# A cross-attention and mixture-of-experts kernel: first units' loads and copies in a new order, and scores and copies moved forward in the units without a value projection

## The chip, the cores and the metric

The kernel runs on one core of a Trainium2 chip. The metric is device time in microseconds (us) of one execution. One profiled execution is there too, with a record of every instruction. The engines are PE (TensorE; PEld is its weight load), ACT (ScalarE), DVE (VectorE), POOL (GpSimd) and SP, which here only issues DMAs. Each engine executes its own list in order.

## The reference, cut to what matters

```python
x = x + _L0_xattn_ref(_layernorm(x, axis=-1), ctx_1024, ctx_1024, L0_xattn_WQ, L0_xattn_WK, L0_xattn_WV, L0_xattn_Wfc, L0_xattn_bfc)
x = x + _L0_ffn_ref(_layernorm(x, axis=-1), L0_ffn_gate_w, L0_ffn_Wg, L0_ffn_Wu, L0_ffn_Wd, L0_ffn_Ws_g, L0_ffn_Ws_u, L0_ffn_Ws_d)
```

There are 32 sequences of 100 tokens with 512 features. `_L0_xattn_ref` projects the normalised x to queries and the first 100 rows of the context to keys and values, takes a causal softmax in 16 heads of 32 features, multiplies it with the values, and projects the result with `Wfc`. `_L0_ffn_ref` sends the 12 best tokens of each sequence to each of 16 experts and adds a shared expert. The change lies in the attention alone; the second line is unchanged.

## The kernel before, in words

**Units.** The attention runs in 32 units. Unit u stands for super-block sb = u // 4 (four sequences, 400 tokens) and feature chunk c = u % 4 (128 features, four heads). The main loop (L561) issues units 0 to 28; `last_units` (L421) writes out 29 to 31 together with the start of the feed-forward part. All five engines' orders are written out by hand: the order of the calls is the order of the instructions on each engine.

**Three units at once.** Iteration u works on three units: the query projection `qproj(u)` of its own, scores and softmax of a = u - 1, and transposes and value product of back = u - 2. For a: `scores(a)` (L259, PE, into the one score tile, `sc`), `sm_max` (L270, DVE) in two halves of two sequences each, `sm_sub` (L279, POOL), `sm_exp` (L285, ACT), `sm_sum` (L290 and L291, DVE) and `sm_mul` (L296, POOL). For back: `p_turn` (L302, PE transposes of one sequence's probabilities into a PSUM tile `ms`), `p_keep` (L307, ACT, copy of that tile to `pt`), and `values` (L317, PE, into another `ms` tile). `y_keep` (L104 on ACT, L105 on DVE) copies the value product out one iteration later and writes it to `yD`. There are two `ms` buffers: the transposes of sequences 2 and 3 take those of sequences 0 and 1, the value product takes that of sequence 2, and the next unit's second transpose takes that of the value product.

**Keys and values beside it.** The context comes in nine blocks j of 2 or 3 times 128 rows. Blocks 0 and 1 are projected in `prologue` (L332), the seven others in iterations 1 to 28, four iterations a block: each has one key projection (`kproj`, copied by `kkeep`, L223, to `kD` in memory) and the first three also have a value projection (`vproj`, copied by `vkeep`, L203, to `vD`). The fourth, u = 4, 8, ..., 28, is a unit without values. `ctx_split` (L138 on ACT, L139 on POOL, tile `cxl`) prepares a later block. `kload` (L229) and `vload` (L234) read keys and values back; `xt_load`, `xt_split`, `x_load`, `x_stats` and `x_rstd` (L161, L162 on POOL) prepare queries and the normalisation of a later super-block. The projections share two PSUM buffers `kv`, so each waits for the copy of the one two before it.

**Order in a unit without values, before.** ACT: `q`, exponential of half 0 of a, `pt` of sequences 0 and 1, exponential of half 1, `pt` of sequences 2 and 3, `kk`. PE: `scores(a)`, `qproj`, transposes 0 and 1, `kproj`, transposes 2 and 3, `values`. POOL: two `sm_sub`, `x_rstd` (every fourth unit), two `sm_mul`, `cxl`, and then the next unit's `sm_sub`.

**Queue of loads.** SP issues nearly all DMAs in the order of the program, and an issue waits for the completion of the DMA eight places before it, besides its own data. `last_units` uses the output projection `fc` (L56, with tiles `yh` and `yl`, loaded by `load_y`, L1048) from its first unit on; `vload` of the last super-block stands in `last_units` (L437).

Of the kernel before, what the change touches and what calls it, by code (L numbers as in the profile page):

```python
# [18 lines left out]
NC4 = D // 128  # L19
# [41 lines left out]
def attention(tc, K, F):  # L61
    nc = tc.nc
    with ExitStack() as ctx, ExitStack() as kvctx:
# [37 lines left out]
        nsb = K.nsb  # L101
# [31 lines left out]
        def ctx_split(j, d, eng=nc.gpsimd):  # L133
            n = KVB[j] * 128
            cr = cur.pop(("cr", j, d))
            h = cxp.tile([128, KMAX], FR, name="cxh")
            l = cxp.tile([128, KMAX], FR, name="cxl")
            nc.scalar.copy(h[:, 0:n], cr[:, 0:n])  # L138
            eng.tensor_tensor(l[:, 0:n], cr[:, 0:n], f32(h[:, 0:n]), ALU.subtract)  # L139
            cur.setdefault(("ch", j), []).append(h)  # L140
            cur.setdefault(("cl", j), []).append(l)
# [22 lines left out]
        def xt_load(sb, d):  # L164
            r = xrp.tile([128, SB], F32, name="xr")
            nc.sync.dma_start(r, K.xC[d, :, sb * SB:(sb + 1) * SB])
            cur["xr", sb, d] = r
# [58 lines left out]
        def kload(u):  # L226
            sb, c = divmod(u, NC4)
            kt = ktp.tile([128, SB], F32, name="kt")
            nc.sync.dma_start(kt, K.kD[:, c, sb * SB:(sb + 1) * SB])  # L229
            cur["k", u] = kt  # L230
# [98 lines left out]
        NU = nsb * NC4  # L329
        blocks = range(2, len(KVB))  # L330

        def prologue():  # L332
            nc.gpsimd.dma_start(mask, K.mask)
            nc.vector.memset(avg, 1.0 / D)
            zp = ps_ms.tile([128, NC4, 128], F32, name="ms")
            for _ in range(WARM):
                nc.tensor.matmul(zp[:, 0, :], avg, avg, start=True, stop=True)
            wk = [load_wc(0, 0)]
            for d in range(NC4):
                ctx_load(0, d)  # L340
            wk += [load_wc(0, c) for c in range(1, NC4)]
            wv = [load_w(1, 0), load_w(1, 1)]
            split_wc(0, 0, wk[0])
            for d in range(NC4):
                ctx_split(0, d, nc.vector)
            wv.append(load_w(1, 2))
            p0 = kproj(0, 0)
            split_wc(0, 1, wk[1])
            wv.append(load_w(1, 3))
            kkeep(0, 0, p0)  # L350
            p0 = kproj(0, 1)
            split_wc(0, 2, wk[2])
            split_wc(0, 3, wk[3])
            for d in range(NC4):
                ctx_load(1, d)
            wq = [load_wc(2, 0)]
            kkeep(0, 1, p0)
            p0 = kproj(0, 2)
            split_w(1, 0, wv[0])
            split_w(1, 1, wv[1])  # L360
            for d in range(2):
                xt_load(0, d)
            kkeep(0, 2, p0)
            p0 = kproj(0, 3)
            split_w(1, 2, wv[2])
            split_w(1, 3, wv[3])
            wq.append(load_wc(2, 1))
            kkeep(0, 3, p0)
            p0 = vproj(0, 0)
            for d in range(NC4):  # L370
                ctx_split(1, d, nc.vector)
            for d in range(2):
                xt_split(0, d)
                xt_load(0, d + 2)
            vkeep(0, 0, p0)
            p0 = vproj(0, 1)
            for d in range(NC4):
                ctx_load(2, d)
            wq += [load_wc(2, 2), load_wc(2, 3)]
            vkeep(0, 1, p0)  # L380
            for c in range(NC4):
                kkeep(1, c, kproj(1, c))
                if c == 0:
                    wq_sum(0, wq[0])
                    wq_sum(1, wq[1])
                    kload(0)
                    for b in range(4):
                        x_load(0, b)
                else:
                    ctx_split(2, c - 1)  # L390
                if c == 1:
                    wq_mean(0)
                    wq_keep(0, wq[0])
                    xt_split(0, 2)
                if c == 2:
                    xt_split(0, 3)
                    wq_mean(1)
                    wq_keep(1, wq[1])
                if c > 1:
                    wq_sum(c, wq[c])  # L400
            xt_load(1, 0)
            ctx_load(3, 0)
            vkeep(1, 0, vproj(1, 0))
            return wq

        def turns(u, *bs):
# [14 lines left out]
        def last_units(pr):  # L421
# [12 lines left out]
                pr.load_x(i)  # L434
            y_keep(u - 3)
            kload(u + 1)
            vload(nsb - 1)  # L437
            maxes(u - 1)
            qkeep(u, qproj(u))
            turns(u - 2, 0, 1)  # L440
# [117 lines left out]

        with tc.manual_schedule(engines={mybir.EngineType.Pool}):
            wq = prologue()  # L560
            for u in range(NU - 3):  # L561
                sb, c = divmod(u, NC4)
                a, back = u - 1, u - 2
                a = a if a >= 0 else None
                back = back if back >= 0 else None
                j, ck = divmod(u - KS, NC4)
                j += 2
                kv = j in blocks
                vv = kv and ck < KVB[j]
                jn, d = divmod(u + NC4 - KS, NC4)  # L570
                jn += 2
                jl, dl = divmod(u + NC4 + 2 - KS, NC4)
                jl += 2
                xs = sb + 1 < nsb
                xn = divmod(u + 3, NC4)
                if u > 0:
                    kload(u)
                if jl in blocks and (jl, dl) != (3, 0):
                    ctx_load(jl, dl)
                if u + 4 < NU:  # L580
                    x_load(*divmod(u + 4, NC4))
                if u + 5 < NU:
                    xt_load(*divmod(u + 5, NC4))
                if u in FC_AT:
                    fr = load_w(3, FC_AT.index(u))
                if u == FC_AT[-1] + 1:
                    F.load_consts()
                if u == FC_AT[-1] + 4:
                    F.split_consts()
                if a is not None:  # L590
                    scores(a)
                if u - 3 >= 0:
                    y_keep(u - 3)
                if a is not None:
                    sm_max(a, 0)
                    sm_sub(a, 0)
                    sm_max(a, 1)
                    sm_sub(a, 1)
                if xs:
                    xt_split(sb + 1, c)  # L600
                qkeep(u, qproj(u))
                if u == 0:
                    for b in range(3):
                        x_stats(0, b)
                    wq_mean(2)
                    wq_mean(3)
                if u == 1:
                    wq_keep(3, wq[3])
                if a is not None:
                    sm_exp(a, 0)  # L610
                if back is not None:
                    p_turn(back, 0)
                    p_turn(back, 1)
                    p_keep(back, 0)
                    p_keep(back, 1)
                x_stats(*xn)
                if xn[1] == 3:
                    x_rstd(xn[0])
                if a is not None:
                    sm_exp(a, 1)  # L620
                    sm_sum(a, 0)
                    sm_mul(a, 0)
                pk = kproj(j, ck) if kv else None
                if kv and vv:
                    kkeep(j, ck, pk)
                if c == 1:
                    vload(sb)
                if back is not None:
                    p_turn(back, 2)
                    p_turn(back, 3)  # L630
                    p_keep(back, 2)
                    p_keep(back, 3)
                if kv and not vv:
                    kkeep(j, ck, pk)
                if a is not None:
                    sm_sum(a, 1)
                    sm_mul(a, 1)
                if jn in blocks:
                    ctx_split(jn, d)
                if u in FC_AT:  # L640
                    F.fc_split(FC_AT.index(u), fr)
                if u == 0:
                    wq_keep(2, wq[2], nc.gpsimd)
                    vkeep(1, 1, vproj(1, 1))
                if vv:
                    vkeep(j, ck, vproj(j, ck))
                if back is not None:
                    values(back)
            kvctx.close()
            F.open_first()  # L650
            pr = F.prep(0, lambda: ps_kv.tile([128, D], F32, name="kv"),
                        lambda: ps_ms.tile([128, NC4, 128], F32, name="ms"))
            pr.load_y()
            last_units(pr)


# [705 lines left out]
```

## Time and profile before

| What | us |
|---|---|
| median of three runs | 1669.77 (1668.22 to 1671.05) |
| the profiled execution | 1668.51 |
| its span, first to last instruction | 1666.7 |
| PE busy in the span | 1641.7 (98%) |
| ACT busy | 695.9 (42%) |
| DVE busy | 916.7 (55%) |
| POOL busy | 627.6 (38%) |
| attention: PE idle in 20 to 372 us | about 18.4 |
| mean granted PE clock | 0.999 of full speed |

The last row but one is the length of the windows from 20 to 372 us less PE's busy time in them. A line of the timeline has the start, the duration, the engine, the line of the kernel, the operation, what it writes and reads, and the shapes; what stands in square brackets is idle time of the engine just before it and what ended that. A line of waits has the waiting engine and line, what it waited for, the total in us, how often, and the longest. Feed-forward work starts on PE at 362.2 us.

### The profile page before, as it was taken

To read this page: it belongs to the slowest core of one execution; us is meant where nothing else is said; L and a number is where in the kernel's file an instruction comes from. 1 tells how busy PE (TensorE), PEld (TensorE's weight loads), DVE (VectorE), ACT (ScalarE), POOL (GpSimd) and SP (SyncE) were. 2 spreads that over 40 slices of the span, in tenths; PEclk is the share of its full clock that TensorE was granted. 3 is DMA by queue.
4 is the path that set the end of the run, shared out by engine and by line. 5 is a ranking of instruction groups with operands and counts; after the bars stand their busy time and mean duration, and the time that the engine had idled before them with its cause. 6 is when DMAs were issued, how large, how long until landed. Compare 5 with 4: busy or idle time off the path is not lost.

```text
span 1666.7 us, 27942 instructions
## 1 busy us (share of the span) xinstructions
PE 1641.7 (98%) x10722; PEld 1503.5 (90%) x10722; DVE 916.7 (55%) x2175; ACT 695.9 (42%) x1152; POOL 627.6 (38%) x502
## 2 busy tenths in 40 slices
PE   8999999999999999999999999999999999999999
PEld 7788888879989998999999999999999999999998
DVE  5778777665433434343665555555555555555542
ACT  4666666553111111112444444444444444444442
POOL 1878777680110011010653344443344343344001
PEclk9999999999999999999999999999999999999999
DMA  7566655565312223211455555455555455555452
GB/s 236 167 188 204 196 176 169 194 192 187 114 62 84 76 90 126 82 46 41 155 172 161 161 167 154 153 150 161 163 160 161 153 149 163 163 155 163 138 160 61
DMA packets 113637, 244.02 MB, mean 146 GB/s; under 512 B 16625, under 2 KB 64978, under 8 KB 113504
## 3 DMA queue, kind: packets, MB, share of 16 engines
q1 hardware_dynamic: 100000, 216.54, 39.7%
q0 software_dynamic: 13088, 25.22, 7.9%
q8 instruction: 84, 1.38, 0.3%
q10 hardware_dynamic: 416, 0.48, 0.1%
q14 instruction: 49, 0.40, 0.1%
HBM read 188.46 MB, written 53.73 MB: 145 GB/s over the span
## 4 chain that ended last, share of the span: by engine, by line
PE 91%; DVE 2%; ACT 2%; POOL 2%; DMA 1%; issue 1%; SPq 0%; ACTq 0%; POOLq 0%; DVEq 0%
PE gu L56 49%; PE dn L56 24%; PE kv L56 9%; PE m L56 3%; PE ms L302 2%; PE ms L317 2%; POOL p L279 1%; PE sc L259 1%; DVE p L270 1%; ACT p L285 1%; ACT pt L307 1%; DMA xr<-xT 1%; DVE y L105 0%; DMA raw<-wA 0%; PE m L1143 0%
## 5 line engine op out<-in xcount | busy, mean ns | idle before, releaser
L56 PE MATMUL gu<-xh,whl 128*128 128x384 f32 (+1 forms) x3200 | 641.3, 332 | 0.0
L56 PEld LDWEIGHTS gu<-xh,whl 128*128 128x128 f32 x3200 | 555.8, 188 | 20.3 <-issue 1.3
L967 POOL DMA_INDIRECT gx<-xnD,iq x192 | 245.4, 1278 | 395.4 <-DVE big L1010 296.3
L56 PE MATMUL dn<-whl,hh 128*128 128x512 f32 x1168 | 366.3, 395 | 0.0
L770 DVE TENSOR_TENSOR whl<-wraw,whl 128x1536 fp32r<-128x1536 f32 x142 | 249.7, 1759 | 197.7 <-ACT whl L769 197.7
L56 PE MATMUL gu<-xl,whl 128*128 128x384 f32 (+1 forms) x1600 | 335.8, 331 | 0.0
L56 PEld LDWEIGHTS gu<-xl,whl 128*128 128x128 f32 x1600 | 279.1, 188 | 0.0
L804 ACT CAST hh<-g 128x384 fp32r<-128x384 f32 (+1 forms) x200 | 101.0, 505 | 407.6 <-DVE g L801 407.6
L56 PEld LDWEIGHTS dn<-whl,hh 128*128 128x128 f32 x1168 | 215.7, 188 | 35.7
L801 DVE TENSOR_TENSOR g<-g,gu 128x384 f32<-128x384 f32 (+1 forms) x200 | 108.2, 541 | 253.6 <-PE gu L56 247.3
L769 ACT CAST whl<-wraw 128x1536 fp32r<-128x1536 f32 x142 | 209.8, 1477 | 56.1 <-PE dn L56 53.1
L56 PE MATMUL dn<-whl,hl 128*128 128x512 f32 x584 | 230.5, 395 | 0.0
L800 ACT ACTIVATE g<-gu 128x384 f32<-128x384 f32 (+1 forms) x200 | 96.2, 481 | 232.6 <-PE gu L56 232.5
L805 DVE TENSOR_TENSOR hl<-g,hh 128x384 fp32r<-128x384 f32 (+1 forms) x200 | 111.6, 558 | 114.2 <-ACT hh L804 114.2
L1022 POOL DMA_INDIRECT out_dram<-x,isl x48 | 77.7, 1619 | 171.0 <-ACT x L1021 161.3
L56 PEld LDWEIGHTS dn<-whl,hl 128*128 128x128 f32 x584 | 109.6, 188 | 26.0
L279 POOL TENSOR_TENSOR p<-p,mx 100x800 f32<-100x800 f32 x64 | 105.7, 1672 | 43.0 <-DVE mx L270 42.4
L296 POOL TENSOR_TENSOR p<-p,sm 100x800 f32<-100x800 f32 x64 | 97.2, 1524 | 29.1 <-DVE sm L291 27.8
L270 DVE CUSTOM_DVE_ANT_0 p<-sc,mask 100x100 f32<-100x100 f32 x512 | 95.3, 256 | 0.0
L1059 POOL TENSOR_TENSOR x<-x,bfc 128x512 f32<-128x512 f32 x23 | 30.6, 1354 | 154.7 <-DMA x<-x 154.7
L285 ACT ACTIVATE p<-p,rstd 100x400 f32<-100x400 f32 x128 | 73.7, 624 | 20.3 <-POOL p L279 20.3
L1011 ACT CAST xh<-big 128x512 fp32r<-128x512 f32 x59 | 36.6, 621 | 101.1 <-DVE big L1010 101.1
(158 smaller groups left out, 1579.3 us busy)
## 6 DMA issues: line engine op xcount, KB each, us to landing
wraw<-wE SPq DMA_DIRECT2D x144, 768.0 KB
yD<-y SPq DMA_DIRECT2D x31, 400.0 KB
xr<-xT SPq DMA_DIRECT2D x32, 200.0 KB
vD<-vt SPq DMA_DIRECT2D x25, 256.0 KB
kt<-kD SPq DMA_DIRECT2D x32, 200.0 KB
v<-vD SPq DMA_DIRECT2D x8, 800.0 KB
xnD<-xn SPq DMA_DIRECT2D x25, 256.0 KB
out_dram<-x SPq DMA_DIRECT2D x25, 256.0 KB
```

The costliest lines, as they stand in the source:

```text
L56: r = nc.tensor.matmul(out, t[0][a], t[1][b], start=(first and i == 0), stop=(last and i == n - 1))
L270: nc.vector.tensor_tensor_reduce(out=p[:, bb, h, :], in0=sc[:, h, cs], in1=mask, scale=ISCALE, scalar=NEG, op0=ALU.add, op1=ALU.max, accum ...
L279: nc.gpsimd.tensor_tensor(pv, pv, mx[:, :, None].to_broadcast([S, 8, S]), ALU.subtract)
L285: nc.scalar.activation(p[:, bb], p[:, bb], AF.Exp, scale=rstd[:, b:b + 1])
L296: nc.gpsimd.tensor_tensor(pv, pv, sm[:, :, None].to_broadcast([S, 8, S]), ALU.mult)
L769: nc.scalar.copy(h, r)
L770: nc.vector.tensor_tensor(l, r, f32(h), ALU.subtract)
L800: nc.scalar.activation(g[:, 0:t], pg[:, 0:t], AF.Gelu)
L801: nc.vector.tensor_tensor(g[:, 0:t], g[:, 0:t], pu[:, 0:t], ALU.mult)
L804: nc.scalar.copy(hh[:, 0:t], g[:, 0:t])
L805: nc.vector.tensor_tensor(hl[:, 0:t], g[:, 0:t], f32(hh[:, 0:t]), ALU.subtract)
L967: nc.gpsimd.indirect_dma_start(out=g[:, k, :], out_offset=None, in_=self.K.xn.rearrange("t (a f) -> (t a) f", f=128), in_offset=bass.Indir ...
```

## The change

1. **Prologue.** `kload(0)` moves behind `xt_load(1, 0)`, and `x_load(1, 0)` is issued just after it. `ctx_split(2, 0)` moves from c = 1 to c = 3, `ctx_split(2, 1)` and `(2, 2)` behind the value projection of block 1.
2. **Units 0 to 2.** `xt_split(1, 0)` goes from ahead of `qproj(0)` to the end of unit 0. The exponentials of unit 0 stand behind the key projection (half 0) and behind the value projection (half 1) of iteration 1, and the value projection stands ahead of the second; in iteration 2 the exponential of half 0 stands behind the `pt` copies of sequences 0 and 1. `x_load` and `x_stats` run one unit further ahead throughout, so `x_rstd` falls in the unit ahead of the one without values.
3. **Units without values** (`nov`). The exponential of half 1 moves behind the `pt` copies of sequences 2 and 3. Except in u = 28, `scores(u)` moves from the start of the next unit to ahead of `values`; in that next unit `y_keep` stands behind the first `sm_max` and `sm_sub`.
4. **Unit 28.** `vload` of the last super-block moves here, ahead of `load_y`.

```diff
@@ prologue
                 if c == 0:
                     wq_sum(0, wq[0])
                     wq_sum(1, wq[1])
-                    kload(0)
                     for b in range(4):
                         x_load(0, b)
-                else:
-                    ctx_split(2, c - 1)
+                if c == 3:
+                    ctx_split(2, 0)
...
             xt_load(1, 0)
+            kload(0)
+            x_load(1, 0)
             ctx_load(3, 0)
             vkeep(1, 0, vproj(1, 0))
+            ctx_split(2, 1)
+            ctx_split(2, 2)
             return wq
@@ last_units
             kload(u + 1)
-            vload(nsb - 1)
             maxes(u - 1)
@@ main loop
-                xn = divmod(u + 3, NC4)
+                xn = divmod(u + 4, NC4) if u + 4 < NU else None
+                nov = kv and not vv
...
-                if u + 4 < NU:
-                    x_load(*divmod(u + 4, NC4))
+                if u + 5 < NU:
+                    x_load(*divmod(u + 5, NC4))
...
-                if a is not None:
+                if a is not None and not ahead:
                     scores(a)
-                if u - 3 >= 0:
+                if u - 3 >= 0 and not ahead:
                     y_keep(u - 3)
                 if a is not None:
                     sm_max(a, 0)
                     sm_sub(a, 0)
+                    if ahead:
+                        y_keep(u - 3)
                     sm_max(a, 1)
                     sm_sub(a, 1)
-                if xs:
+                if xs and u > 0:
                     xt_split(sb + 1, c)
                 qkeep(u, qproj(u))
                 if u == 0:
-                    for b in range(3):
+                    for b in range(4):
                         x_stats(0, b)
+                    x_rstd(0)
...
-                if a is not None:
+                if a is not None and u > 2:
                     sm_exp(a, 0)
...
+                if u == 2:
+                    sm_exp(a, 0)
-                x_stats(*xn)
-                if xn[1] == 3:
-                    x_rstd(xn[0])
-                if a is not None:
+                if xn:
+                    x_stats(*xn)
+                    if xn[1] == 3:
+                        x_rstd(xn[0])
+                if a is not None and u > 1 and not nov:
                     sm_exp(a, 1)
                     sm_sum(a, 0)
                     sm_mul(a, 0)
                 pk = kproj(j, ck) if kv else None
                 if kv and vv:
                     kkeep(j, ck, pk)
+                if u == 1:
+                    sm_exp(a, 0)
+                    sm_sum(a, 0)
+                    sm_mul(a, 0)
+                if nov:
+                    sm_sum(a, 0)
+                    sm_mul(a, 0)
...
+                if u == 1:
+                    vkeep(j, ck, vproj(j, ck))
+                if u == 1 or nov:
+                    sm_exp(a, 1)
                 if kv and not vv:
                     kkeep(j, ck, pk)
...
-                if vv:
+                if vv and u > 1:
                     vkeep(j, ck, vproj(j, ck))
+                if u == 0:
+                    xt_split(1, 0)
+                if u == NU - 4:
+                    vload(nsb - 1)
+                ahead = nov and u < NU - 4
+                if ahead:
+                    scores(u)
                 if back is not None:
                     values(back)
```

## The prediction, as it was put on record

> **What bounds the kernel now.** I read the waits of PE by stage first, then the busy time by window. After 372 us no PE matmul waits for another engine. The columns of the windows are: stretch, its length, busy time and instructions of PE, PEld, DVE, ACT and POOL, granted clock, DMA share, GB/s.
>
> ```profile
> 38.00:43.00 5.00, 4.66 (x44) 4.00 (x44) 4.86 (x21) 1.39 (x4) 1.37 (x3) 0.67 0.19 63
> ...
> 440.00:700.00 260.00, 260.00 (x1394) 235.17 (x1393) 101.15 (x176) 44.31 (x89) 31.23 (x46) 1.00 0.27 89
> ...
> 1300.00:1640.00 340.00, 340.00 (x1814) 318.05 (x1813) 184.60 (x201) 153.09 (x203) 109.91 (x81) 1.00 0.53 153
> ```
>
> From 440 us on PE is busy the whole stretch, so I take it that whatever PE gains or loses before 372 us arrives at the end one for one. All PE waits that can go are in the attention. In 20 to 60 us, and then in 60 to 372 us:
>
> ```profile
> PE sc L259 <- ACT q L249: 2.8, 1, 2.8
> PE ms L302 <- ACT pt L307: 1.5, 1, 1.5
> PE kv L56 <- ACT kk L223: 1.3, 1, 1.3
> PE kv L56 <- ACT q L223: 1.2, 2, 0.7
> PE kv L56 <- ACT vt L203: 0.5, 1, 0.5
> ```
>
> ```profile
> PE ms L317 <- ACT pt L307: 7.6, 9, 1.3
> PE ms L317 <- DMA v<-vD: 1.8, 1, 1.8
> ```
>
> The first list sums to 7.3 us. Seven of the nine L317 waits are 0.86 us each, one in each unit without values, 6.0 us together. So the three things that the change touches hold 7.3 + 6.0 + 1.8 = 15.1 us, and the slowed clock in 38 to 43 us besides. The question is which of these waits end, and which only move.
>
> **Units 0 to 2: about 4.6 us gained.** Before, SP stands from 23.7 to 28.3 us at `kload(0)`, waiting for the write of the keys; DMAs fall idle (82 GB/s in 27 to 28, none in 28 to 29), `xr` is issued at 31.72 and lands at 37.1, and ACT, with the copy of `xr` ahead of that of `q`, holds PE 2.81 us until 38.09. After, four loads of x fill that hole and `xr` is copied later. I follow the new order in the durations of the old rows. ACT copies `q` of the keys without the two `cxh` ahead of it, so the L223 waits (0.47 and 0.71) go and `qproj(0)` runs at 28.3 instead of 29.52. Bytes in the queue: from 27.25 four x loads (0.82 MB at about 0.27 MB/us, the rate of 30 to 32 us) to 30.3, three key writes (0.39 MB at about 0.195, as in 32 to 34) to 32.3, `xr` 32.9, `kt` 33.5, `xt` 34.1; with 1.5 us from last byte to use, as `xr` had, `kt` is there at 35.0 and `xt` at 35.6. Scores then run at 35.0, not 38.09. New on DVE: the statistics of `xt` (0.87) stand ahead of the L189 subtraction for the third weight chunk, and behind that wait ACT's `wh` and `vt` copies: 35.6 + 0.87 + 0.67 + 0.6 + 0.6 gives `kproj(2, 0)` at 38.3 instead of 43.21, 4.9 us early. Then something is late next: `xnl` of (1, 0) now stands ahead of `sm_max`, which runs 39.25 to 42.15; the fourth chunk's L189 and `wh`, then `kk`, end at 44.35; `qproj(2)` waits about 0.1. The first exponential is done at 45.4, its sum 46.65, its product 48.3, so the first transposes wait from 46.7 to 48.35 and `kproj(2, 1)` starts at 48.97, not 53.47: 4.5 early. The 1.50 us wait for `pt` goes, but the exponentials of unit 1, ahead of `kk` and the next `pt` copies, end at 55.5, and `values(0)` starts at 56.3, not 60.88: **-4.6 us**. Ends: -7.3 - 1.2 (all waits and the half clock gone) is -8.5; if `kt` or `xt` lands 3 us later than I have it, -1.5. No row shows this queue order, hence the width.
>
> The clock: in 40 to 43 us PE was granted 0.50, after the idle 2.81 us, and eight matmuls took 2.66 us of pitch where they take 1.46, so about 1.2 us went; the idle times of 1.33 and 1.50 us brought none. [...]
>
> **Units without values: about 5.8 us lost.** The unit at 112 us and the one after it, on PE, ACT and POOL:
>
> ```profile
> 119.95 0.89 PE L317 MATMUL ms<-pt,v 100*32 100x100 f32 x32 [0.86 <-ACT pt L307]
> ...
> 126.81 0.94 PE L302 MATMUL ms<-ident,p 100*100 100x100 f32 x8
> ```
>
> ```profile
> 118.37 1.15 ACT L285 ACTIVATE p<-p,rstd 100x400 f32<-100x400 f32 x2
> 119.42 0.87 ACT L307 COPY pt<-ms 100x400 f32<-100x400 f32 x2
> ...
> 125.23 1.15 ACT L285 ACTIVATE p<-p,rstd 100x400 f32<-100x400 f32 x2 [0.57 <-POOL p L279]
> 126.29 0.86 ACT L307 COPY pt<-ms 100x400 f32<-100x400 f32 x2
> ```
>
> ```profile
> 119.62 3.00 POOL L296 TENSOR_TENSOR p<-p,sm 100x800 f32<-100x800 f32 x2
> 122.59 1.01 POOL L139 TENSOR_TENSOR cxl<-cr,cxh 128x384 fp32r<-128x384 f32 x1
> 123.67 3.34 POOL L279 TENSOR_TENSOR p<-p,mx 100x800 f32<-100x800 f32 x2
> ```
>
> The wait goes: the transposes start at 118.23, the copies can follow 0.6 us later (as at 366.52 and 367.12), at 118.84, and scores (0.89) cover what is left; PE enters the next unit 0.86 early. But the exponential moved from 118.37 to 118.84 + 0.76 = 119.6, 1.23 later. Behind it: DVE's sum (0.99 + 0.20) ends at 122.07 instead of 120.84; POOL's second product starts 0.18 later, at 122.25, where it started at 121.1 (behind `rstd`, which leaves this unit: no more than 0.3 us of slack there). `cxl` and the next unit's L279 stand behind it: L279 starts at 122.25 + 1.47 + 1.08 = 124.8 (was 123.67), the exponential at 126.36, `pt` at 127.42. The second transposes need those `pt` copies to free their `ms` tiles, 0.52 after the first copy starts: 127.94, where they ran at 126.81. Before, that copy was just in time (PE idle there under 0.1 us), so there is no slack: the wait of 0.86 turns into one of about 2.0, and PE is 1.13 us late. The moved `y_keep` holds the second transpose to about 124.1, 0.65 us, hidden in the larger wait. Moving scores alone gains nothing while the copy sets the pace. Nothing later pays it back: the units that follow have no PE idle time. Five of six times 1.13, and 0.2 in unit 17, where a DVE operation of 1.45 us already held the same chain (PE waited 0.98): **+5.8 us**. Ends: -5.2 (all six 0.86 gone) and 6 x 1.5 = +9. I take the chain, since each link is a row.
>
> **Last super-block: about 4.5 us lost.** SP's issues, then PEld and PE:
>
> ```profile
> 322.42 0.39 SPq L1048 DMA_DIRECT2D yh<-yD  x1
> 322.89 0.53 SPq L1048 DMA_DIRECT2D yl<-yD  x1
> ...
> 327.21 0.31 SPq L234 DMA_DIRECT2D v<-vD  x1
> ```
>
> ```profile
> 329.34 0.75 PEld L56 LDWEIGHTS kv<-wfh,yl 128*128 128x128 f32 x4 [0.42 <-DMA yl<-yD]
> ```
>
> ```profile
> 340.61 0.89 PE L317 MATMUL ms<-pt,v 100*32 100x100 f32 x32 [1.77 <-DMA v<-vD]
> ```
>
> The 1.77 us wait goes: `v` will be there early. But `v` (0.8 MB) now stands ahead of `yh` and `yl` (0.79 MB each), and these were just in time: bytes moved from 322.5 reach the end of `yh` at 326.35 and of `yl` at 328.33, and `yl` was used at 329.3, 1.0 later; by the same step `yh` landed at 327.3, when `fc` began (327.24). At 0.25 to 0.3 MB/us `v` puts 2.7 to 3.3 us ahead, and the exponential ahead of `kk` delays the first issue by 0.45. So `fc` starts at about 330.9 (+3.7), after 4.7 us idle, longer than the 2.81 that brought the half clock: about +1.5 (as the 1.2 above), so scores of unit 29 are 5.2 late. At the value product of 340.61 PE is 5.2 - 1.77 = 3.4 late; but the softmax chain of units 29 and 30, which moves with those scores and already holds the product at 350.76 by 1.27 us, is still 5.2 late. Ends: -2.6 (this wait and the 0.86 of unit 28 gone, `yh` unharmed) and +7. Between 3.4 and 5.2 I take **+4.5 us**.
>
> **Sum.** -4.6 + 5.8 + 4.5 = +5.7 us. On the profiled execution's 1668.51 this is 1674.2. That execution lies 1.26 below the median of the runs, 1669.77; against the median the forecast is 1675.5, and I put 1675.
>
> **Rivals.**
> *All waits go* (-4.6 - 5.2 - 2.6 = -12.4: about 1657.4; with only the tail as forecast, about 1664.5). For it: each wait named in the lists is addressed by a move. Against it: the rows at 126.29 and 126.81 leave no slack. It decides if the second transposes after a unit without values start by 126.0 in the old time.
> *Even*: the units without values break even and `yh` waits no more than the old `v` wait took, with the first units at -3 to -4.6 and the tail at +2 to +4: about 1668 to 1671.
> *First units gain nothing*, as `kt` lands late: +5.8 + 4.5 = about 1680. For it: the load of keys is the last of nine now; against it: before, DMAs were idle for over 1 us there.
> That the change does not do what it says is excluded: the order of instructions has it on each engine.
>
> **Numbers.** Forecast 0.50 (own range 1671 to 1680), all waits go, wholly or in part, 0.25, even 0.15, first units gain nothing 0.10. This measurement can tell about 0.2%, 3.3 us, from no change. Slower 0.54 (the forecast without its lowest part, and the last rival), same 0.22, faster 0.24. Range 1661 to 1682: it leaves out the full gain and a tail at its upper end.
>
> **What would show it.** After: PE waits at L317 for `pt` fall from nine to two or three, and six new ones of 1.3 to 2.2 us stand at L302 in units 5, 9, ..., 25 (unit 17 too). A PE wait at L56 with `yh` of some 4 us before 332, none at L317 for `v`, and a clock below 0.9 after it. Scores of unit 0 near 35. I am wrong if L302 shows no such waits, or if `yh` lands by 328.

## The result and the profile after

The changed kernel takes 1679.33 us (median of five runs, 1678.36 to 1680.07), the kernel before 1669.77 in the runs beside it: a ratio of 1.0056, 95% interval [1.0042, 1.007], or 9.6 us slower, 0.6%. The profiled execution took 1678.60 us, its span 1676.6, PE busy 1645.3 of it. The forecast of 1675 had the sign and two of its three steps in size; the third, the last super-block, cost twice what it was given.

The granted clock and the busy time in three windows of the kernel after (columns as in the windows shown of before):

```profile
38.00:43.00 5.00, 5.00 (x26) 4.28 (x25) 4.24 (x34) 1.65 (x4) 3.04 (x3) 1.00 0.64 205
326.00:338.00 12.00, 6.01 (x25) 4.66 (x23) 4.03 (x24) 4.04 (x9) 6.05 (x4) 0.62 1.02 324
440.00:700.00 260.00, 260.00 (x1401) 234.97 (x1400) 100.95 (x176) 44.25 (x90) 32.24 (x47) 1.00 0.27 88
```

The half clock of 38 to 43 us is gone (1.00 where it was 0.67), and a new one stands at 326 to 338, where PE is busy for half of the stretch. From 440 us on PE is busy all the time, as before, so the whole difference lies ahead of it. PE's waits of the kernel after, in 20 to 60 us and in 60 to 380 us:

```profile
PE ms L302 <- POOL p L296: 1.6, 1, 1.6
PE sc L259 <- DMA kt<-kD: 1.5, 1, 1.5
PE ms L317 <- ACT pt L307: 1.3, 1, 1.3
PE kv L56 <- ACT kk L223: 0.4, 1, 0.4
```

```profile
PE ms L302 <- ACT pt L307: 7.4, 8, 1.1
PE kv L56 <- DMA yh<-yD: 5.6, 1, 5.6
PE ms L317 <- ACT pt L307: 3.5, 4, 2.6
PE ms L302 <- DVE y L105: 3.2, 6, 0.7
```

In the first stage 7.3 us of waits became 4.8. In the second, the nine L317 waits became four, the wait for `v` went, and L302 has eight waits for `pt` and six for `y`, where it had two (1.4 us) and none before; one transfer, `yh`, costs 5.6 us, nearly as much as the seven waits of 0.86 us of the units without values did (6.0).

The start of the same PE instruction, after less before, tells where each microsecond went. It is one profiled execution against the other:

| PE instruction | before | after | offset | step since the row above |
|---|---|---|---|---|
| scores in iteration 3 | 61.71 | 57.42 | -4.29 | first units -4.29 |
| second transposes in iteration 25 | 288.08 | 288.96 | +0.88 | units without values +5.17 |
| second transposes in unit 29 | 326.50 | 326.83 | +0.33 | wait in unit 28 shorter (0.86 to 0.29): -0.55 |
| first `fc`, with `yh` | 327.24 | 333.30 | +6.06 | wait for `yh`: +5.73 |
| value product behind `fc` | 330.47 | 338.71 | +8.24 | `fc` at half clock: +2.18 |
| value product that waited for `v` | 340.61 | 347.51 | +6.90 | wait 1.77 for `v` to 0.29 for `pt`: -1.34 |
| next value product | 350.76 | 359.15 | +8.39 | wait for `pt` 1.27 to 2.58, and 0.2: +1.49 |
| `fc` behind it | 353.16 | 363.00 | +9.84 | lowered clock again: +1.45 |
| last value product | 369.76 | 379.57 | +9.81 | |

So -4.3, +5.2 and, from unit 28 on, +8.9.

**A unit without values, after.** PE, ACT and POOL at the same place as the rows shown of before, which lie about 2.1 to 3.1 us later in the old time:

```profile
116.80 0.89 PE L317 MATMUL ms<-pt,v 100*32 100x100 f32 x32
...
120.94 0.55 PE L302 MATMUL ms<-ident,p 100*100 100x100 f32 x4 [0.51 <-DVE y L105]
...
124.74 0.94 PE L302 MATMUL ms<-ident,p 100*100 100x100 f32 x8 [1.14 <-ACT pt L307]
```

```profile
116.50 1.16 ACT L285 ACTIVATE p<-p,rstd 100x400 f32<-100x400 f32 x2
...
123.16 1.15 ACT L285 ACTIVATE p<-p,rstd 100x400 f32<-100x400 f32 x2 [2.55 <-POOL p L279]
124.21 0.86 ACT L307 COPY pt<-ms 100x400 f32<-100x400 f32 x2
```

```profile
119.15 1.53 POOL L296 TENSOR_TENSOR p<-p,sm 100x800 f32<-100x800 f32 x1 [1.54 <-DVE sm L291]
120.64 1.00 POOL L139 TENSOR_TENSOR cxl<-cr,cxh 128x384 fp32r<-128x384 f32 x1
121.60 3.34 POOL L279 TENSOR_TENSOR p<-p,mx 100x800 f32<-100x800 f32 x2
```

The value product waits no more (116.80 has no bracket). But from the late exponential at 116.50 the row of links runs on: POOL, which went straight on to its second product in the rows of before, waits there 1.54 us for DVE's sum; `cxl` and the subtraction follow back to back; ACT waits 2.55 us for them; and PE's second transposes wait 1.14 us for ACT's copies, after 0.51 us for the moved `y_keep`. In place of 0.86 us stand 1.65.

**The last super-block, after.** SP's issues, PE's two waits that the lowered clock follows (0.50 in 330 to 338 and in 360 to 362), and the piece of the chain of waits between them (start, length, what):

```profile
323.77 0.32 SPq L234 DMA_DIRECT2D v<-vD  x1
324.15 0.49 SPq L1076 DMA_DIRECT2D yh<-yD  x1
324.73 0.46 SPq L1076 DMA_DIRECT2D yl<-yD  x1
```

```profile
333.30 2.07 PE L56 MATMUL kv<-wfh,yh 128*128 128x512 f32 x4 [5.60 <-DMA yh<-yD]
...
359.15 1.26 PE L317 MATMUL ms<-pt,v 100*32 100x100 f32 x32 [2.58 <-ACT pt L307]
```

```profile
324.15 9.11 DMA yh<-yD
```

Before, `yh` was issued at 322.42 and used at 327.24, 4.8 us later; now it is issued at 324.15 and takes 9.1. In the three windows of 2 us from 324 to 330, with `v` ahead, the DMAs moved 149, 227 and 249 GB/s; in 332 to 336, when `yh` had landed or was about to, 370 and 377. In the kernel before, 324 to 328 had 305 and 399.

### The profile page after: what moved, and what is told of

Same layout as the page of the kernel before. It is cut to its first block, busy times and chain, and to the rows that moved or that the text cites. A ratio compares the mean times of both kernels' runs of the same rounds, so it can differ in the third digit from the quotient of the medians.

```text
span 1676.6 us, 27939 instructions
## 1 busy us (share of the span) xinstructions
PE 1645.3 (98%) x10722; PEld 1505.0 (90%) x10722; DVE 917.1 (55%) x2175; ACT 697.3 (42%) x1152; POOL 627.5 (37%) x502
## 4 chain that ended last, share of the span: by engine, by line
PE 93%; DMA 2%; ACT 1%; DVE 1%; POOL 1%; issue 1%; SPq 0%; ACTq 0%; POOLq 0%; DVEq 0%
PE gu L56 49%; PE dn L56 24%; PE kv L56 10%; PE m L56 3%; PE ms L302 2%; PE ms L317 1%; PE sc L259 1%; POOL p L279 1%; DMA yh<-yD 1%; ACT p L285 1%; DMA p<-x 0%; DMA xr<-xT 0%; DVE p L270 0%; ACT pt L307 0%; POOL cxl L139 0%
## 5 line engine op out<-in xcount | busy, mean ns | idle before, releaser
L797 ACT CAST whl<-wraw 128x1536 fp32r<-128x1536 f32 x142 | 209.8, 1477 | 56.3 <-PE dn L56 53.2
L290 DVE TENSOR_REDUCE sm<-p 100x8 f32<-100x800 f32 x64 | 63.1, 986 | 34.4 <-ACT p L285 33.5
```

Of the source, the lines that this page charges most:

```text
L797: nc.scalar.copy(h, r)
```

## The experiments

Twelve kernels, each compared with the kernel before on the same chip; a delta is its median less the median of before beside it (1669.56, 1669.49 and 1670.37 in the three groups, so that medians of different groups can be off by about 1 us against each other). The first four do one part of the change alone.

**First units alone** (`p_only`): the changed prologue, units 0 to 2 and the loads one unit further ahead; the rest as before. Against the changed kernel:

```diff
             kload(u + 1)
+            vload(nsb - 1)
...
-                nov = kv and not vv
+                nov = False
...
-                if u == NU - 4:
-                    vload(nsb - 1)
```

> The kernel before with the new order of the prologue and of units 0 to 2 alone (and the loads and statistics of x one unit further ahead). My account: scores of unit 2 stood at 61.71 before and at 57.42 after the change, and nothing behind them gives that back, so 4.3 us less: about 1665.5. Rival: the gain is lost again later, where other queues meet a PE that is early: 1669 to 1670.

Measured 1665.77 (1664.42 to 1666.31), ratio 0.9975 [0.9965, 0.9986], -3.8 us. In its profile PE is 3.93 us early in unit 28 and 2.43 early at the last value product: the difference is a clock of 0.83 and then 0.89 in 344 to 356, behind a wait of 1.64 us. Behind the next value product `p_only` needs 20.49 us to the last one, where the kernel before needs 19.00. The gain is real and comes through, less what the clock takes.

**`v` ahead of `yh` alone** (`v_only`), against the kernel before, as the next two:

```diff
             kload(u + 1)
-            vload(nsb - 1)
...
+                if u == NU - 4:
+                    vload(nsb - 1)
```

> The kernel before with the load of the last values moved ahead of the loads of yh and yl, alone. My account: fc waits 4 to 6 us for yh, the PE clock is halved behind that wait, and the wait for v of 1.77 us goes: 8 to 9 us more, about 1678. Rival (yh would not have been hurt but for the units without values, which came late): 1.8 us less, about 1668.

Measured 1677.66 (1675.07 to 1679.12), ratio 1.0046 [1.0032, 1.0059], +8.1. PE waits 4.73 us for `yh` and the clock is 0.76 in 328 to 330 and 0.50 in 330 to 334:

```profile
332.62 2.07 PE L56 MATMUL kv<-wfh,yh 128*128 128x512 f32 x4 [4.73 <-DMA yh<-yD]
```

The one line that ends a wait of 1.77 us costs 8.1 us; the rest of the change, taken together, costs 1.5.

**The exponential behind the copies alone** (`e_only`):

```diff
+                nov = kv and not vv
...
-                    sm_exp(a, 1)
+                    if not nov:
+                        sm_exp(a, 1)
...
+                if nov:
+                    sm_exp(a, 1)
```

> The kernel before with the exponential of half 1 behind the pt copies in units without values, alone. My account: the wait for pt at the value product falls from 0.86 to about 0.3 us, but the transposes of the next unit wait about 1.7 us for the pt copies behind its first exponential; 1.0 us more in five of six pairs of units, none in unit 17: about 5 us more, 1675. Rival (copies early are gained): 7 times 0.57 us less, about 1666.

Measured 1675.79 (1674.44 to 1677.39), ratio 1.0038 [1.0024, 1.0052], +6.2. The L317 waits fall from 0.86 to 0.29, and waits of 1.47 for `pt` stand at the next unit's second transposes, six times, as here:

```profile
130.59 0.94 PE L302 MATMUL ms<-ident,p 100*100 100x100 f32 x8 [1.47 <-ACT pt L307]
```

`fc` waits 0.89 for `yh` in this kernel too: in unit 28 the exponential stands ahead of `kk`, whose write heads SP's queue.

**Scores ahead alone** (`s_only`), and with them `y_keep` behind the first `sm_max` and `sm_sub` in the next unit:

```diff
-                if a is not None:
+                if a is not None and not ahead:
                     scores(a)
...
+                ahead = kv and not vv and u < NU - 4
+                if ahead:
+                    scores(u)
                 if back is not None:
                     values(back)
```

> The kernel before with scores ahead of the value product in units without values (and the copy of the value product behind the first maximum in the next unit), alone. My account: the 0.86 us wait at the value product goes, and the second transposes of the next unit wait as much, since the pt copies ahead of them are no earlier: within 1 us of before, 1669 to 1671. Rival (the gain stays): six times 0.86 us less, about 1664.6.

Measured 1668.68 (1666.95 to 1671.81), ratio 0.9994 [0.9985, 1.0003], -0.9: not to be told from no change. The six waits of 0.86 are gone, and 0.63 to 0.67 for `pt` stand in the next unit, five times, as here; in unit 17 it is 1.12 for `y`:

```profile
126.48 0.94 PE L302 MATMUL ms<-ident,p 100*100 100x100 f32 x8 [0.63 <-ACT pt L307]
```

The wait moved, without the exponential being late; that it is by the same chain as the forecast's is shown further down (`psvc`).

The four deltas sum to -3.8 + 8.1 + 6.2 - 0.9 = +9.6, the whole change. Each delta has an interval of about 1.5 to 2.5 us to either side, so that the sum meets the whole to a tenth is luck; that it meets it within the noise means that no part needs another for its loss.

**`v` earlier still** (`a_vtop`): the changed kernel, `v` asked for at the start of unit 28, where the DMAs of the changed kernel stand at 0 to 11 GB/s (318 to 324 us).

```diff
+                if u == NU - 4:
+                    vload(nsb - 1)
                 if u in FC_AT:
...
-                if u == NU - 4:
-                    vload(nsb - 1)
                 ahead = nov and u < NU - 4
```

> The changed kernel with the load of the last v issued at the very start of unit 28, ahead of the loads of that unit, where the trace shows SP's queue and the DMAs idle (10 and then 0 GB/s in 318 to 322), so that it no longer stands ahead of yh and yl. Theory (v ahead of yh costs the tail +9.0, by delay and by the slowed clock behind it): the wait for yh returns to under 0.5 us, the clock stays at 1.00 in 326 to 364, the wait for v stays away, and the time falls by 9 to 10.8 us, to 1668.5 to 1670.5. Rival (the moved exponential of unit 28 makes yh late, not v): the wait for yh stays above 2 us and the time falls by less than 4, to 1675 or more.

Measured 1672.72 (1670.06 to 1675.82), ratio 1.0019 [1.001, 1.0028], 6.6 us less than the changed kernel: between the two theories, 2 short of the first. The wait for `yh` fell from 5.60 to 0.95, so `v` in the queue made 4.7 of it (4.73 in `v_only`) and the exponential 0.9 (0.89 in `e_only`). The first theory had under 0.5 there. What it missed besides is the other end: with `v` early, the next wait for `pt` stays at 2.58, and the clock drops behind it (0.68 in 350 to 360). This profiled execution, of 1674.89, is one of the slowest of its eleven runs; in it the clock also falls in 20 to 30 us (0.83, where the changed kernel has 1.00), with a wait of 2.4 us for `vt`.

**`v` behind `yh` and `yl`** (`a_vback`):

```diff
-                if u == NU - 4:
-                    vload(nsb - 1)
...
             pr.load_y()
+            vload(nsb - 1)
             last_units(pr)
```

> The changed kernel with one line moved: the load of the last v directly behind yh and yl instead of ahead of them, still in unit 28 and 9 us before the value product that reads it. Theory (what hurts is only that its 0.8 MB stand ahead in the same queue): yh waits some 0.9 us, as it does with the moved exponential alone, no wait for v, about 1672.5, the same as with v at the start of the unit. Rival (the transfers share the DMA engines, so v delays yh and yl wherever it is issued near them): a wait for yh or yl of over 2.5 us and 1676 or more.

Measured 1676.03 (1675.14 to 1680.57), ratio 1.0035 [1.0023, 1.0047]. Both theories fell: the rival's wait of over 2.5 us for `yh` or `yl` is not there, and the first theory's time is not either. PE's rows in its profiled execution, at 1680.57 the longest of its runs, so that the second wait may be shorter in the others:

```profile
331.36 1.20 PE L56 MATMUL kv<-wfh,yh 128*128 128x512 f32 x4 [0.83 <-DMA yh<-yD]
...
339.67 1.67 PE L259 MATMUL sc<-kt,q 32*100 32x100 f32 x32 [3.67 <-DMA kt<-kD]
```

`yh` is nearly in time, as the first theory had it, but the load of keys that follows in the queue is now behind `v`, and scores wait 3.67 us for it and take 1.67 us for 0.96, at a lowered clock (0.90 in 330 to 340, 0.76 in 340 to 350). Ahead of `yh` and behind `yl`, what stands next behind `v` is late. At its old place, behind that load of keys, no PE wait for a later load follows, and `v` itself is late by 1.77.

**Matmuls in place of the wait for `yh`** (`a_fill`):

```diff
+            pr.fill(0, 18)
             pr.fc(0)
...
+    def fill(self, i, n):
+        F = self.F
+        self.ps[i] = self.pm()
+        for _ in range(n):
+            F.nc.tensor.matmul(self.ps[i], F.wfh[:, 0, 0:128], F.wfh[:, 0, :], start=True, stop=True)
...
```

> The changed kernel with 18 matmuls of 128x512 on resident tiles (0.26 us each, 4.7 us) put on PE ahead of the first output projection, where PE stands idle for yh for 5.6 us; they write the tile that the projection overwrites, so nothing of the result comes from them. Theory (of the loss in the last super-block, the wait for yh is one part and the clock of 0.50 behind it another, 2.2 us there and 1.4 at the next wait): yh still lands when it did, the projection takes 3.2 us rather than 5.4, the clock is above 0.95 in 328 to 340, and the time is about 2.2 us less, 1677. Rival (the clock does not matter for the end, since the softmax chain behind it sets the pace): no difference, 1679.

Measured 1677.24 (1675.98 to 1680.28), ratio 1.0047 [1.0033, 1.0061], 2.1 less than the changed kernel, which the two intervals do not tell from nothing. The size is near the theory's, the profile is not: `yh` came 1.6 us later than in the changed kernel (`fc` at 334.88), and after the fill PE still stood 3.04 us, and the clock fell again for the first matmuls of `fc` (0.62 in 334 to 336; 4.35 us for all of it, between the 3.2 and 5.4 of before and after). Behind the next wait, of 2.58, the clock stayed at 1.00. The test is not clean and settles little; the one below is.

**The exponential back, scores ahead, `v` at the top** (`psv`) and, besides, **`cxl` out of the chain** (`psvc`). Against the changed kernel, the second has all of this:

```diff
+                if u == NU - 4:
+                    vload(nsb - 1)
...
-                if a is not None and u > 1 and not nov:
+                if a is not None and u > 1:
                     sm_exp(a, 1)
...
-                if nov:
-                    sm_sum(a, 0)
-                    sm_mul(a, 0)
...
-                if u == 1 or nov:
+                if u == 1:
                     sm_exp(a, 1)
...
-                if jn in blocks:
+                if jn in blocks and (d < 3 or jn == 2):
                     ctx_split(jn, d)
+                if jn in blocks and jn > 2 and d == 2:
+                    ctx_split(jn, 3)
...
-                if u == NU - 4:
-                    vload(nsb - 1)
```

and the first all but the lines with `jn`.

> The changed kernel with the exponential, sum and product of half 1 back at their old place in the units without values, and the load of the last v at the start of unit 28: so the new prologue and units 0 to 2, and scores ahead of values. Theory: the first units give their 3.9 us, scores ahead give 0 to 1, the wait of 1.77 for v goes: 1669.6 - 3.9 - 0.5 - 1.5 is about 1663.5. Rival (the wait for v only moves to the next wait for pt, as 3.9 us of the first units partly did): 1665.5.

> As the kernel with the new first units, scores ahead and v at the start of unit 28, and besides the split of the fourth piece of each context block moved one iteration earlier, so that POOL's cxl (1.0 us) leaves the chain from the second product to the next unit's subtraction in the units without values. Theory (that chain, cxl in it, holds the next exponential, its copies and the second transposes, so that scores ahead could not give their 0.86): the waits of 0.65 at the second transposes of the next unit go, and the time is 3 to 4 us below that kernel's, near 1660. Rival (another link, DVE's sum or ACT's own order, holds the same copies): the waits stay within 0.2 us and so does the time; or the moved split makes the iteration before late by as much.

Measured 1665.21 (1663.87 to 1665.72), ratio 0.9969 [0.9957, 0.9981], and 1660.67 (1658.94 to 1661.08), ratio 0.9943 [0.993, 0.9957]. For `psv` the rival was right: without the wait for `v` the next wait for `pt` is 2.58. For `psvc` the theory was: 4.5 us less from one split moved. The second transposes at the same place, `psv` first:

```profile
123.74 0.94 PE L302 MATMUL ms<-ident,p 100*100 100x100 f32 x8 [0.58 <-ACT pt L307]
```

```profile
120.97 0.85 PE L302 MATMUL ms<-ident,p 100*100 100x100 f32 x8
```

The bracket is gone, in all six units behind one without values. The rival's other clause, that the moved split makes the iteration before late, came true once: a new wait of 0.69 at 153.07. So POOL's chain, with `cxl` in it, was what turned the gain of scores ahead into a wait.

**The same with the late exponential** (`a_vtop_c`): `a_vtop` with the split moved in the same way.

> The changed kernel with v at the start of unit 28 (1672.72 measured) and the fourth split of each context block one iteration earlier, the exponential still behind the pt copies. Theory (the late exponential costs its unit through POOL's chain of second product, cxl and subtraction, and through nothing else): without cxl's 1.0 us in it the waits of 1.14 for pt at the second transposes go, 5 x 1.0 us, about 1667.5. Rival (ACT's own order or DVE's sum holds them): no change, 1672.7.

Measured 1666.93 (1664.12 to 1669.65), ratio 0.9983 [0.9974, 0.9992], 5.8 less than `a_vtop` by the medians, 6.7 by the deltas. The waits of 0.99 to 1.14 for `pt` fell to 0.17 to 0.27, as here; those of 0.5 to 0.8 for `y` stayed:

```profile
122.54 0.86 PE L302 MATMUL ms<-ident,p 100*100 100x100 f32 x8 [0.23 <-ACT pt L307]
```

So the exponential's harm came through that chain.

**`v` back at its old place** (`psc`): `psvc` without the early load.

> The best kernel so far (new first units, scores ahead, split moved, v at the start of unit 28: 1660.67) with the load of the last v back at its old place. Theory (the wait for v runs beside the softmax chain of units 29 and 30, so that ending it only lengthens the next wait for pt, from about 1.3 to 2.6 us): within 1 us of it or up to 1.5 less, as the waits are shorter and the clock is less often lowered: 1659 to 1661. Rival (the wait for v is a loss of its own): 1662.2 or more.

Measured 1658.58 (1657.99 to 1659.51), ratio 0.9929 [0.9915, 0.9942]: no slower than `psvc`, 2.1 us lower by the medians, 3.0 by the deltas, and just below the theory's 1659 to 1661. The value products of `psvc` and of `psc`:

```profile
340.59 1.56 PE L317 MATMUL ms<-pt,v 100*32 100x100 f32 x32 [2.57 <-ACT pt L307]
```

```profile
330.53 0.89 PE L317 MATMUL ms<-pt,v 100*32 100x100 f32 x32 [1.54 <-DMA v<-vD]
...
340.92 0.89 PE L317 MATMUL ms<-pt,v 100*32 100x100 f32 x32 [1.52 <-ACT pt L307]
```

Two waits of 1.5, or one of 0.29 (at 328.95) and one of 2.57: the sums are 3.06 and 2.86. Counted from the second transposes of unit 29, PE reaches the later product after 24.17 us in `psc` and 24.48 in `psvc`. The wait for `v` runs beside the softmax chain and is worth next to nothing; ending it makes one long wait of two short ones.

**Matmuls in place of that wait** (`psvc_fill`): `psvc` with nine matmuls ahead of the product that waits 2.57.

```diff
+        def sc_fill(n):
+            sc = cur["scf"] = ps_sc.tile([S, 4, D], F32, name="sc")
+            for _ in range(n):
+                nc.tensor.matmul(sc[:, 0, :], F.wfh[:, 0, 0:S], F.wfh[:, 0, :], start=True, stop=True)
...
             pr.pt = mt
+            sc_fill(9)
             values(u - 2)
```

> The best kernel so far (1660.67) with 9 matmuls of 100x512 on resident tiles (some 2.2 us) on PE ahead of the value product that waits 2.57 us for pt; they write the score tile, which the next scores overwrite, so nothing of the result comes from them. Theory (behind that wait the clock falls to 0.50 and the next 5 us of work take 2.8 us more in the profiled execution): the wait with the fill in it is as long, the clock stays at 1.00, and the time is 1.4 to 2.8 us less: about 1658.5. Rival (the lowered clock there belongs to the profiled execution, or is paid back behind it): no difference, 1660.7.

Measured 1658.20 (1657.83 to 1659.35), ratio 0.9928 [0.9914, 0.9941], 2.5 less than `psvc` by the medians, 3.35 by the deltas; the two intervals overlap in part. The windows from 340 to 344 us, `psvc` first; the last three columns are granted clock, DMA share and GB/s:

```profile
340.00:344.00 4.00, 3.41 (x56) 2.79 (x60) 2.57 (x5) 2.17 (x6) 3.05 (x2) 0.50 0.70 242
```

```profile
340.00:344.00 4.00, 3.52 (x74) 2.60 (x73) 3.41 (x8) 3.22 (x8) 3.05 (x2) 1.00 0.84 281
```

From the product behind the wait to the last value product `psvc` needs 21.59 us, `psvc_fill` 18.99 and `psc` 18.95: the lowered clock takes 2.6 us, and work of no use on PE saves it. This is not of one execution alone: the mean granted clock is 1.000 in all five runs of `psvc_fill` and 0.997 to 0.999 in those of `psvc`. The fill itself delays nothing: the product comes 24.20 us after the second transposes of unit 29, against 24.48. `psc` and `psvc_fill` are the best two kernels, faster than both before and after, and cannot be told apart.

## Why the prediction was right, and where its size was off

**First units, -4.6.** Right, at -4.29 in the profile and -3.8 alone. Its times held one by one: scores at 35.05 (35.0 forecast), the first key projection of block 2 at 38.35 (38.3), the transposes at 48.85 (48.35), the value product at 56.59 (56.3); `qproj(2)` waited 0.43 where 0.1 was forecast. The half clock went with the 2.81 us wait (1.00 in 38 to 43 us).

**Units without values, +5.8.** Right in mechanism, +5.17 in the profile: +1.0 to +1.2 in five units and -0.09 in unit 17, where +1.13 and +0.2 were forecast. The wait has the two parts that were named, but they add up instead of the smaller hiding in the larger: 0.51 for `y` and then 1.14 for `pt`. That the chain through `cxl` carries it was only read off the rows then; `psvc` and `a_vtop_c` show it, where taking 1.0 us out of that chain ends or nearly ends the waits for `pt`. That scores ahead alone gain nothing while the copy sets the pace was right as well (`s_only`).

**Last super-block, +4.5.** Here the size failed: +8.9. The term is "between 3.4 and 5.2 I take +4.5 us". First, both ends were low: `v` puts 4.7 us ahead of `yh`, not 2.7 to 3.3, since the DMAs moved 0.15 to 0.25 MB/us in 324 to 330, not 0.25 to 0.3; the exponential adds 0.9, not 0.45; and the half clock takes 2.2, not 1.5. Second, the lower end counted the end of the 1.77 us wait as a gain. The prediction itself said that the chain behind it stays late; had it followed its own sentence, it would have taken the upper end, 5.2: the next wait, 2.58 instead of 1.27, takes back what the end of this one gives. `psc` shows that this wait is worth next to nothing. Third, it did not see that the clock falls behind that longer wait too (0.50 in 360 to 362, 1.45 us). The upper end with 2.0 more for the wait for `yh`, 0.7 more for the half clock and 1.45 for the second one, less 0.55 of unit 28, is 8.8.

**The proofs named.** The L317 waits are four where two or three were named, the new waits in the units after those without values sum to 1.65 in each where 1.3 to 2.2 was named, `yh` waits 5.6, until 333.3, where "some 4" before 332 was, the wait for `v` is gone, and the clock is 0.62 in 326 to 338.

**The rivals.** All waits go: its condition, second transposes by 126.0 in the old time, was not met. Yet most of its price could be had: with the split moved and the exponential and `v` back at their places, `psc` is 11.8 us faster than before by the medians, and 9.8 by the spans of the two profiled executions (1656.9 against 1666.7), whose clocks are nearly alike; that rival had -12.4. The wait for `v` still stands in `psc`. What the rival lacked was a move that the change does not make. First units gain nothing, "about 1680": the time it gives is nearest to what was measured, 1679.33, and its reason is excluded by `p_only`. A right time would have been no proof of it.

**What stays open.** Whether a wait of 1.6 to 2.6 us lowers the clock in a given execution is not settled (below), and with it 1 to 3 us of several of these times. The runs' mean clocks go with it: of the eleven runs of `a_vtop` the one at 1.000 took 1670.06 us and the three at 0.996 took 1675.3 in the mean; of the sixteen of the kernel before beside `psc`, the four at 0.999 took 1668.5 in the mean and the nine at 0.997 took 1670.6. The profiled execution of before, at 0.999, is one of the former, so part of the lead of `psc`, at 1.000 in four runs of five, is that its clock falls less often.

## What to carry to other kernels

When a wait at one instruction is ended by a move in an in-order engine, follow what now stands behind the moved instruction through every engine until the next unit: here the 0.86 us came back there as 1.65, and one POOL operation of 1.0 us, moved out of that chain, was worth 4.5 us over six units. Before a load is issued earlier to end a wait, count its bytes against each load behind it that is just in time, and ask whether another chain ends at the same moment; here a wait of 1.77 us was worth next to nothing and ending it cost 8. Judge an order part by part: the parts' deltas added up to the whole within the noise, and one of the four, the first units, gained by itself. Scores ahead gained nothing by themselves; the kernels that gained most have them together with the moved split, and the split without them was not run.

## What the runs showed of the hardware

- **The clock falls behind short waits too, and not always.** The granted clock dropped behind PE waits of 1.62 (0.72 in 350 to 356, `s_only`), 1.64 (0.83 in 344 to 350 and 0.89 in 350 to 356, `p_only`) and 2.54 to 2.58 us (0.50 in 340 to 344 in `psvc`, 0.95 in 340 to 372 in `psv`, 0.50 in 360 to 362 in the changed kernel, 0.68 in 350 to 360 in `a_vtop`, 0.83 in 360 to 370 in `a_vback`, and `a_vtop_c` with 0.83 in 346 to 350 and 0.74 in 350 to 354), and stayed at 1.00 behind 2.57 in `v_only`, 2.58 in `a_fill`, both waits of 1.5 in `psc` and 1.70 in `e_only`. In `a_vtop` it fell besides in 20 to 30 us (0.83), with a wait of 2.4 us for `vt`. From the value product behind the wait to the last one PE needs 18.95 to 19.00 us at full clock (five kernels besides `psc`), 20.4 to 20.5 with one lowered stretch of about 3.4 us (the changed kernel, `p_only`, `s_only`, `psv`), and 21.6 and 21.75 with one of about 7 (`psvc`, `a_vtop`), so the price is 1.4 to 2.8 us each time. In the clock records the lowered stretch of the kernel before is 3.41 us long (39.70 to 43.12), and those of the changed kernel are 10.24 (328.81 to 339.05, the wait for `yh` and the `fc` behind it) and 3.41 (359.53 to 362.94). The lengths in the other kernels are estimates from the clocks of the windows, with the clock taken as 1.00 or 0.50, as in those records: for `psvc` 0.98, 0.50 and 0.66 in the three windows of 4 us from 336 to 348, for `a_vtop` 0.68 and 0.97 in the two of 10 us from 350 to 370. Why the clock falls behind a wait in one execution and not behind an equal one in another is not shown here.
- **Useless matmuls in the wait are worth their place.** Nine of them, 2.35 us, kept the clock at 1.00 and saved 2.6 us in the profile (`psvc_fill`). In the wait for `yh`, 18 left 3.04 us uncovered, and the clock fell all the same (0.62 in 334 to 336, `a_fill`).
- **Loads differ in rate.** In `a_vtop`, `v` is issued at 318.27, ahead of one write of `yD`, and SP issues nothing more until 325.33. In 320 to 322 and 322 to 324, with these two in the queue, the DMAs moved 224 and 179 GB/s at DMA shares of 0.68 and 0.67. The changed kernel has 249 in 328 to 330, with `v` ahead, and 370 in 332 to 334, at 1.03 and 1.06. So 0.8 MB of `v` hold the queue longer than 0.8 MB of `yh`. Why is not shown here.
